# Side work of a second attention layer: the distance between users of one PSUM bank, by what reads the bank

## The chip, the cores and the metric

The kernel runs on one core of a Trainium2 chip. The metric is the device time of one execution in microseconds (us); lower is better. Given are three timed runs of the kernel before, and one execution that the hardware profiler recorded.

## The reference, cut to what matters

The program is a stack of four transformer layers over 2 sequences of 1024 tokens with 256 features: each layer normalises x, and adds an attention-like part and a feed-forward part to it. The change touches the attention of the second layer alone. It has 16 query heads of 128 dimensions and 4 key/value heads, rotary position embedding, a causal softmax, and a gate per token and head:

```python
q = (hidden_states @ Wq.T).reshape(b, sl, H, D)      # H = 16, D = 128
k = (hidden_states @ Wk.T).reshape(b, sl, HKV, D)    # HKV = 4
v = (hidden_states @ Wv.T).reshape(b, sl, HKV, D)
q = _rope(q, cos, sin); k = _rope(k, cos, sin)
...
scores = jnp.einsum('bhsd,bhtd->bhst', q, k) * scale   # causal
attn = jnp.einsum('bhst,bhtd->bhsd', jax.nn.softmax(scores, axis=-1), v)
out = (g * attn).transpose(0, 2, 1, 3).reshape(b, sl, H * D)
return out @ Wo.T
```

The reference also picks key blocks, but with 16 of 16 picked this does not alter the result, and the kernel leaves it out.

## The kernel before, in words

All matmuls are in fp32. The second attention runs over 8 groups: 2 sequences times 4 key/value heads, each with 4 query heads j. A group goes over 8 tiles of 128 query rows, qt, in the order 7, 0, 6, 1, 5, 2, 4, 3. One *unit* is one pair (qt, j), so there are 32 units in a group and 256 in all, and 7 more at the end that hold only what is left over.

In its unit a pair gets its **scores** on TensorE (PE): `scores()` multiplies 128 query rows with (qt+1)·128 keys into `sc`, a PSUM tile of two banks, of which there are two (`bufs=2`). `softmax()` then adds the causal mask on VectorE (DVE, L156), reduces the maximum there (L158), and takes the exponential with the row sum on ScalarE (ACT, L159), which is the last to read `sc`. A reciprocal on DVE (L666) and a multiplication by it and by the gate on GpSimd (POOL, L667) finish `pr`.

Two units behind the last of a qt's four pairs, `outputs()` begins to work it off: for each block of 128 keys a `turn` (four PE transposes of `pr` into the tile `tp`, L573, copied to `pT` by ACT or DVE in turn, L684) and a `product` (one matmul of 512 columns with v into `op`). These pieces are spread over four units; the first one or two are put ahead of a unit's scores (`early`), the rest behind them (`late`). The last product is followed by a copy of `op` to `oT` on ACT (L697), and queues the **output projection** of this qt: `project(oT)`, four matmuls of 256 columns with `w1o` into the bank m1, which one DVE addition to x reads (`add_to_x`, L134).

The **fills** are the side work: the 8 output projections of a group, and the 12 projections of the next group (2 key, 8 query, 2 value). All use one PSUM bank, m1, one after the other. A key or query projection (four matmul records of 512 columns) is read by three DVE operations (`rope`, L597, L599, L600), a value projection (16 records of 128 columns) by one copy on ACT (L632).

The order of all matmuls and transposes of this stage on PE is the order in which the code emits them (`keep_in_program_order`); the other engines' instructions are ordered by the tile scheduler. In each unit, `unit()` does: the unit's early pieces, the scores, at most one fill, and the unit's late pieces. `took` is the estimated PE time of scores and late pieces (0.22 a block of scores, 0.44 a turn, 0.86 a product). A fill is taken if there is one, if `owed`, the time left over against 3.5 a unit, is above zero, and if `since`, the sum of `took` since the last fill, is above 2.2. `since` contains the late pieces of the present unit, though they are emitted behind the fill. Output projections go to the head of the list of fills.

Of the kernel before, what the change touches and what calls it, by code (L numbers as in the profile page):

```python
# [46 lines left out]
def kernel(ctx: ExitStack, tc: tile.TileContext, a: dict, out: bass.AP):  # L47
# [85 lines left out]
    def add_to_x(i, ps):  # L133
        V.tensor_tensor(xs[i], ps, xs[i], ALU.add)  # L134
# [87 lines left out]
    with work_pool("l0") as pool, tc.tile_pool(  # L222
# [26 lines left out]
        def pe(out_, lhsT, rhs, first, last):  # L249
            tc.keep_in_program_order(PE.matmul(out_, lhsT=lhsT, rhs=rhs, start=first, stop=last))  # L250
# [4 lines left out]
        def bank():  # L255
            free.append(free.pop(0))
            return free[-1]
# [134 lines left out]
        def project(b, pair, qt):  # L392
            i = b * QT + qt
            yp = bank()[:, :D]
            for jp in range(2):
                pe(yp, os_[b, pair, jp][:, qt * P : (qt + 1) * P], wo0[:, 2 * pair + jp, :], jp == 0, jp == 1)
            add_to_x(i, yp)
# [32 lines left out]
        begun, soon, later = [], [], []  # L430
# [6 lines left out]
        owed = [0.0]  # L437
# [26 lines left out]
        for b, pair in pairs:  # L464
            for h in range(2):
                for g in (2 * pair, 2 * pair + 1):
                    for qt in range(4 * h, 4 * h + 4):
                        n = (qt + 1) * P
# [93 lines left out]
    with work_pool("l1") as pool, tc.tile_pool(  # L562
# [40 lines left out]
        groups = [(b, g) for b in range(B) for g in range(4)]  # L603
        kTs, qTs, vgs = {}, {}, {}

        def key(b, g, h):
            if (b, g) not in kTs:
                kTs[b, g] = pool.tile([P, T], F32, tag="k1", name=f"kT1_{b}_{g}")
            cols = slice(h * 512, (h + 1) * 512)
            kp = bank()  # L610
            for k in range(2):
                pe(kp, w1k[:, k, g * P : (g + 1) * P], xnT[2 * b + h][:, k, :], k == 0, k == 1)
            rope(kTs[b, g][:, cols], kp, cols, f"k{b}_{g}_{h}")

        def query(b, g, j, h):
            if (b, g, j) not in qTs:
                qTs[b, g, j] = pool.tile([P, T], F32, tag="q1", name=f"qT1_{b}_{g}_{j}", bufs=8)
            hc = slice((4 * g + j) * P, (4 * g + j + 1) * P)
            cols = slice(h * 512, (h + 1) * 512)
            qp = bank()  # L620
            for k in range(2):
                pe(qp, w1q[k][:, hc], xnT[2 * b + h][:, k, :], k == 0, k == 1)
            rope(qTs[b, g, j][:, cols], qp, cols, f"q{b}_{g}_{j}_{h}")
# [10 lines left out]
        def projections(b, g):  # L634
            return (
                [lambda h=h: key(b, g, h) for h in range(2)]
                + [lambda j=j, h=h: query(b, g, j, h) for j in range(4) for h in range(2)]
                + [lambda h=h: value(b, g, h) for h in range(2)]
            )
# [11 lines left out]
        with phase("l1_main") as main:  # L651

            def scores(b, g, qt, j):
                n = (qt + 1) * P
                i = b * QT + qt
                nm = f"1_{b}_{g}_{qt}_{j}"
                sc = main.tile([P, T], F32, tag="S", name=f"sc{nm}", bufs=2)
                for c in range(0, n, 512):
                    cols = slice(c, min(c + 512, n))
                    pe(sc[:, cols], qTs[b, g, j][:, qt * P : n], kTs[b, g][:, cols], True, True)  # L660
                long = n > 512
                pr = pool.tile([P, 512 * (1 + long)], F32, tag=f"pr{long}", name=f"pr{nm}", bufs=7)
                total = pool.tile([P, 1], F32, tag="total", name=f"total{nm}", bufs=4)
                softmax(pool, sc, n, pr[:, :n], total, nm)
                r = pool.tile([P, 1], F32, tag="r", name=f"r{nm}", bufs=4)
                V.reciprocal(r, total)  # L666
                G.tensor_scalar(  # L667
                    pr[:, :n], pr[:, :n], r, gate[:, i, 4 * g + j : 4 * g + j + 1],
                    op0=ALU.mult, op1=ALU.mult,
                )  # L670
                return pr

            def outputs(b, g, qt, prs):

                nm = f"1_{b}_{g}_{qt}"
                made = {}

                def turn(kb):
                    tp = main.tile([P, 4, P], F32, tag="T", name=f"tp{nm}_{kb}", bufs=2)
                    for j in range(4):  # L680
                        pe_t(tp[:, j, :], prs[j][:, kb * P : (kb + 1) * P])
                    made[kb] = pool.tile([P, 4, P], F32, tag="pT1", name=f"pT{nm}_{kb}", bufs=3)
                    with tc.high_priority():
                        (V.tensor_copy if kb % 2 else S.copy)(made[kb], tp)  # L684

                def product(kb):
                    if kb == 0:
                        made["op"] = main.tile([P, 4, P], F32, tag="O", name=f"op{nm}")
                    op = made["op"]
                    pe(  # L690
                        op.rearrange("p j q -> p (j q)"), vgs[b, g][:, kb, :],
                        made[kb].rearrange("p j q -> p (j q)"), kb == 0, kb == qt,
                    )
                    if kb == qt:
                        oT = pool.tile([P, 4, P], F32, tag="oT1", name=f"oT{nm}")
                        with tc.high_priority():
                            S.copy(oT, op)  # L697
                        soon.append((1.75, lambda: project(oT)))

                def project(oT):  # L700
                    yp = bank()[:, :D]
                    for j in range(4):
                        h = 4 * g + j
                        pe(yp, oT[:, j, :], w1o[h // 8][:, h % 8, :], j == 0, j == 3)
                    add_to_x(b * QT + qt, yp)

                pieces = [(0.44, lambda: turn(0))]
                for kb in range(qt + 1):
                    if kb < qt:
                        pieces.append((0.44, lambda kb=kb: turn(kb + 1)))  # L710
                    pieces.append((0.86, lambda kb=kb: product(kb)))
                return pieces

            early, late, soon, fills = {}, {}, [], []
            UNIT, owed, since, u = 3.5, 0.0, 0.0, 0

            def unit(make):
                nonlocal owed, since  # L720
                for _, work in early.pop(u, []):
                    work()
                took, pr = make()
                took += sum(cost for cost, _ in late.get(u, []))
                fills[0:0] = soon
                soon.clear()
                owed += UNIT - took
                since += took
                if fills and owed > 0 and since > 2.2:
                    cost, work = fills.pop(0)  # L730
                    owed -= cost
                    since = 0.0
                    work()
                for _, work in late.pop(u, []):
                    work()
                return pr

            for n, (b, g) in enumerate(groups):
                due = [(1.75, work) for work in projections(*groups[n + 1])] if n + 1 < len(groups) else []
                fills += due  # L740
                for qt in (7, 0, 6, 1, 5, 2, 4, 3):
                    prs = []
                    for j in range(4):
                        prs.append(
                            unit(lambda: (0.22 * (qt + 1), scores(b, g, qt, j)))
                        )

                        if u < NSLOT:
                            tc.keep_in_program_order(
                                nc.scalar.dma_start(out=sent[u * P : (u + 1) * P, :], in_=none)  # L750
                            )
                        u += 1
                    pieces = outputs(b, g, qt, prs)
                    cut = 1 + (qt > 0)
                    early[u + 2], pieces = pieces[:cut], pieces[cut:]
                    share = sum(cost for cost, _ in pieces) / 4
                    for m in range(4):
                        late[u + 2 + m] = []
                    at, used = u + 2, 0.0
                    for piece in pieces:  # L760
                        late[min(at + int(used / share), at + 3)].append(piece)
                        used += piece[0]
                while due and due[-1] in fills:
                    fills.pop(0)[1]()
            while early or late or soon or fills:
                unit(lambda: (2.5, None))
                u += 1
# [37 lines left out]
    with work_pool("l2") as pool, tc.tile_pool(  # L805
# [410 lines left out]
        for blk in range(N2 + 1):  # L1216
            for i in range(4):
                t, hs = i // 2, i % 2
                work = []
# [643 lines left out]
```

## Time and profile before

| | |
|---|---|
| Median of three runs | 3122.94 us (3121.41 to 3129.98) |
| Profiled execution: its time / its span | 3125.69 us / 3124.0 us |
| Second attention's main loop, within the span | 742 to 1656 us |
| PE busy in it | 885.65 us of 914 |
| DVE / ACT / POOL busy in it | 546.04 / 337.58 / 297.75 us |
| Mean granted clock of PE in the whole span / in this stage | 0.97 / 1.00 |
| Matmuls of this stage by kind: scores / products / transposes | 286.1 / 292.9 / 164.7 us |
| Output projections / query, value, key projections | 123.3 / 107.2, 27.9, 24.4 us |

A line of a timeline gives the start, the time, the engine, the line of the kernel, the operation, what it writes and reads, the shape and how many equal instructions follow one another; in square brackets stands how long the engine was idle before, and what ended that. An fp32 matmul shows as two records, so an output projection of four matmuls is "x8". The end of a matmul is modelled, and the next one starts some 0.15 us before it: the time that one takes from its neighbours is the distance between starts. A line of the waits gives who waited for whom, the total in us, how many times, and the longest. A line of stages gives the length, the busy time of each engine with its instruction count, the granted clock, the share of the DMA engines and GB/s.

### The profile page before, as it was taken

What the parts mean: (1) busy time and instruction counts of PE and PEld (TensorE: products, weight loads), DVE (VectorE), ACT (ScalarE), POOL (GpSimd) and SP (SyncE); (2) the same over time, 40 slices, a digit from 0 to 9 for tenths busy, and PEclk for the clock granted to TensorE, in tenths of its full rate; (3) what the DMA queues carried; (4) which work ended last, traced back from release to release, by engine and by line L of the source; (5) the groups of instructions that cost most, each with busy time, mean ns of one, the idle gap of its engine ahead of it and who ended that gap; (6) DMA issues with size and microseconds to landing.
All of it is one profiled execution on the core that took longest, in us unless ns stands there. A gap on an engine that the chain in (4) does not pass through costs nothing. (4 is left out here: it accounts for less than half of the span.)

```text
span 3124.0 us, 43744 instructions
## 1 busy us (share of the span) xinstructions
PE 2911.5 (93%) x16724; PEld 1976.3 (63%) x16724; DVE 1741.7 (56%) x3876; ACT 1194.8 (38%) x2122; POOL 923.1 (30%) x1274
## 2 busy tenths in 40 slices
PE   6999999989999999999999977999999999998798
PEld 5666666545655655655655555677777777655697
DVE  5765655326666666566551167677777775333223
ACT  2123333332333333333441144765766665222111
POOL 2021010103333333333320024444354443212462
PEclk9999999979999999999999988999999999999899
DMA  5000010001100000000000010000000000002496
GB/s 157 1 28 15 1 55 1 1 28 60 40 23 1 1 1 0 1 1 14 35 1 18 1 41 1 1 1 1 1 1 1 1 1 20 17 1 93 157 351 210
DMA packets 77203, 107.76 MB, mean 34 GB/s; under 512 B 7680, under 2 KB 60480, under 8 KB 75456
## 3 DMA queue, kind: packets, MB, share of 16 engines
q1 hardware_dynamic: 62160, 85.05, 8.4%
q10 hardware_dynamic: 11376, 10.41, 1.0%
q0 software_dynamic: 3456, 9.47, 0.8%
q8 instruction: 134, 2.20, 0.3%
q14 instruction: 77, 0.63, 0.1%
HBM read 82.94 MB, written 21.97 MB: 34 GB/s over the span
## 5 line engine op out<-in xcount | busy, mean ns | idle before, releaser
L159 ACT ACTIVATE pr<-sc,nmax 128x896 f32<-128x896 f32 (+7 forms) x272 | 201.3, 741 | 469.2 <-DVE nmax L158 372.3
L667 POOL TENSOR_SCALAR pr<-pr,r,gate 128x1024 f32<-128x1024 f32 (+7 forms) x256 | 209.9, 821 | 564.3 <-DVE r L666 535.3
L570 PE MATMUL sc<-kT,qT 128*128 128x512 f32 (+3 forms) x768 | 291.7, 491 | 22.3 <-ACT pr L159 22.3
L570 PE MATMUL op<-pT,v 128*128 128x512 f32 x576 | 292.9, 595 | 1.8 <-DVE pT L684 1.2
L344 ACT ACTIVATE pT<-sc 128x1024 f32<-128x1024 f32 (+1 forms) x160 | 150.1, 938 | 269.7 <-PE sc L250 269.6
L570 PEld LDWEIGHTS sc<-kT,qT 128*128 128x128 f32 x768 | 138.6, 192 | 156.9 <-issue 123.4
L158 DVE TENSOR_REDUCE nmax<-sc 128x1 f32<-128x896 f32 (+7 forms) x272 | 205.1, 757 | 8.0
L573 PEld LDWEIGHTS tp<-cst,pr 128*128 128x128 f32 x1152 | 140.7, 142 | 99.6 <-issue 70.4
L933 DVE SCALAR_TENSOR_TENSOR xp_ps<-xp,w2r,xp_ps 128x256 f32<-128x256 f32 x320 | 153.5, 486 | 60.3 <-ACT xp_ps L832 52.9
L250 PE MATMUL sc<-qk,qk 32*128 32x256 f32 (+1 forms) x1280 | 167.9, 379 | 9.4 <-ACT pT L344 8.8
L156 DVE TENSOR_TENSOR sc<-sc,cst 128x128 f32<-128x128 f32 x272 | 79.9, 296 | 172.5 <-PE sc L570 157.2
L958 POOL TENSOR_TENSOR dm<-cst,dA 128x512 f32<-128x512 f32 x128 | 133.3, 1050 | 116.2 <-PE lp L826 88.9
L347 POOL TENSOR_SCALAR_AFFINE_SELECT pT<-pT 128x512 f32<-128x512 f32 x64 | 40.6, 635 | 423.7 <-ACT pT L344 420.3
L573 PE MATMUL tp<-cst,pr 128*128 128x128 f32 x1152 | 164.7, 274 | 1.0 <-POOL pr L667 1.0
L250 PE MATMUL mx<-qk,qk 32*128 32x256 f32 (+1 forms) x1280 | 144.6, 387 | 10.8 <-DVE nm L319 3.0
L826 PE MATMUL lp<-dm,cst 128*128 128x512 f32 x256 | 137.1, 653 | 11.3 <-DVE ml L1023 6.4
L250 PEld LDWEIGHTS sc<-qk,qk 32*128 32x128 f32 x1280 | 104.1, 184 | 66.5 <-issue 31.2
L832 ACT ACTIVATE xp<-xp_ps,w2r 128x256 f32<-128x256 f32 x160 | 90.2, 564 | 128.3 <-PE xp_ps L826 104.4
L826 PE MATMUL xp_ps<-xnT,w2x 128*128 128x256 f32 x512 | 131.0, 402 | 7.3 <-DVE xx L933 3.9
L832 ACT ACT_TABLE_LOAD x105 | 134.7, 1283 | 3.7 <-PE zp L826 1.8
L684 ACT COPY pT<-tp 128x512 f32<-128x512 f32 x160 | 93.8, 586 | 106.2 <-PE tp L573 105.9
L826 PE MATMUL op<-w2o,xx 128*128 128x256 f32 x512 | 122.7, 389 | 5.1 <-DVE x L1166 3.7
(322 smaller groups left out, 5979.7 us busy)
## 6 DMA issues: line engine op xcount, KB each, us to landing
we<-in_L_W SPq DMA_DIRECT2D x80, 512.0 KB
sent<-none ACTq DMA_DIRECT2D x47, 129.0 KB
xg<-sent SPq DMA_DIRECT2D x40, 129.0 KB
gu<-in_L_gu SPq DMA_DIRECT2D x4, 1024.0 KB
back<-done SPq DMA_DIRECT2D x16, 256.0 KB
x<-in_x ACTq DMA_DIRECT2D x16, 128.0 KB
dn<-in_L_dn SPq DMA_DIRECT2D x2, 1024.0 KB
tabs<-in_L_rope SPq DMA_DIRECT2D x2, 1024.0 KB
```

Of the source, the lines that this page charges most:

```text
L158: V.tensor_reduce(nmax, sc[:, :n], axis=AX.X, op=ALU.max, negate=True)
L159: S.activation(pr, sc[:, :n], AF.Exp, bias=nmax, accum_out=total)
L250: tc.keep_in_program_order(PE.matmul(out_, lhsT=lhsT, rhs=rhs, start=first, stop=last))
L344: S.activation(pT[:, :, :, :w], sc[:, :, :, :w], AF.Exp, scale=0.25)
L570: tc.keep_in_program_order(PE.matmul(out_, lhsT=lhsT, rhs=rhs, start=first, stop=last))
L573: tc.keep_in_program_order(PE.transpose(out_, in_, ident))
L667: G.tensor_scalar(pr[:, :n], pr[:, :n], r, gate[:, i, 4 * g + j : 4 * g + j + 1], op0=ALU.mult, op1=ALU.mult,)
L684: (V.tensor_copy if kb % 2 else S.copy)(made[kb], tp)
L826: tc.keep_in_program_order(PE.matmul(out_, lhsT=lhsT, rhs=rhs, start=first, stop=last))
L832: tc.keep_in_program_order(S.activation(*args, **kw))
L933: V.scalar_tensor_tensor(dst[:, n] if k == 2 else pp[:, n], xp[:, n, k : k + 256], cw[:, c : c + 1], pp[:, n], op0=ALU.mult, op1=ALU.add,)
L958: G.tensor_tensor(dm, le.unsqueeze(1).to_broadcast([P, 4, P]), dAc[:, 4 * g : 4 * g + 4].unsqueeze(2).to_broadcast([P, 4, P]), ALU.mult,)
```

## The change

A fill now carries its own distance: behind an output projection of outputs the next fill may come once `since` is above 1.3, behind any other projection above 2.2 as before. The distance is set when a fill is taken, and holds for the fill after it. The costs, `owed` and the order of the list are not altered.

```diff
-                        soon.append((1.75, lambda: project(oT)))
+                        soon.append((1.75, lambda: project(oT), 1.3))
...
-            UNIT, owed, since, u = 3.5, 0.0, 0.0, 0
+            UNIT, owed, since, settled, u = 3.5, 0.0, 0.0, 2.2, 0
...
                 since += took
-                if fills and owed > 0 and since > 2.2:
-                    cost, work = fills.pop(0)
+                if fills and owed > 0 and since > settled:
+                    cost, work, settled = fills.pop(0)
                     owed -= cost
                     since = 0.0
                     work()
...
-                due = [(1.75, work) for work in projections(*groups[n + 1])] if n + 1 < len(groups) else []
+                due = [(1.75, work, 2.2) for work in projections(*groups[n + 1])] if n + 1 < len(groups) else []
```

More of the change, by code (lines that the diff above doesn't have):

```diff
@@ L716 @@
             early, late, soon, fills = {}, {}, [], []
-            UNIT, owed, since, u = 3.5, 0.0, 0.0, 0
+            UNIT, owed, since, settled, u = 3.5, 0.0, 0.0, 2.2, 0
             def unit(make):
-                nonlocal owed, since
+                nonlocal owed, since, settled
                 for _, work in early.pop(u, []):
```

## The prediction, made before the changed kernel ran

> **What bounds the kernel now.** I read the page first: TensorE (PE) is busy 93% of the span. Then the busy time by stage, for the second attention's main loop (742 to 1656 us), and what PE waits for in it.
>
> ```profile
> span 3124.0 us, 43744 instructions
> ...
> PE 2911.5 (93%) x16724; PEld 1976.3 (63%) x16724; DVE 1741.7 (56%) x3876; ACT 1194.8 (38%) x2122; POOL 923.1 (30%) x1274
> ```
>
> ```profile
> core 0: us, PE busy (x) PEld busy (x) DVE busy (x) ACT busy (x) POOL busy (x), PEclk, DMA share, GB/s
> 742.00:1656.00 914.00, 885.65 (x3500) 534.51 (x3500) 546.04 (x1165) 337.58 (x749) 297.75 (x326) 1.00 0.03 11
> ```
>
> ```profile
> PE sc L570 <- ACT pr L159: 22.3, 13, 2.3
> ```
>
> The stage is 914 us and PE works 885.65 of it: moving work between units can win back at most the 28.3 us of idle time. Of that, 22.3 us are score matmuls waiting for the exponential (L159) that reads the score buffer they need. The timeline of PE shows this wait once in each of the 8 groups, always 2.30 us: at 782.57, 900.41, 1018.34, 1134.58, 1250.82, 1367.07, 1483.31 and 1588.99, together 18.4 us. The third, in the timeline of PE:
>
> ```profile
> start us, us, engine line op out<-in xcount [idle before <-releaser]
> 1010.71 0.81 PE L570 MATMUL sc<-kT,qT 128*128 128x384 f32 x2
> 1011.36 1.89 PE L570 MATMUL m<-w1o,oT 128*128 128x256 f32 x8
> 1013.08 1.02 PE L570 MATMUL op<-pT,v 128*128 128x512 f32 x2
> 1013.94 2.10 PE L570 MATMUL sc<-kT,qT 128*128 128x512 f32 x6
> 1018.34 0.70 PE L570 MATMUL sc<-kT,qT 128*128 128x256 f32 x2 [2.30 <-ACT pr L159]
> 1018.87 1.89 PE L570 MATMUL m<-w1o,oT 128*128 128x256 f32 x8
> 1020.60 1.04 PE L573 MATMUL tp<-cst,pr 128*128 128x128 f32 x8
> ```
>
> In the code's order, with (qt, head) for the scores, this is: scores (6,2); output projection of qt 7; product of qt 0; scores (6,3) and, in the same row, scores (1,0); the gap; scores (1,1); output projection of qt 0; eight transposes of qt 6. The output projection of qt 0 stands right behind the gap.
>
> **What the change moves.** Nothing is added or removed: 148 fills before and after, with the same matmuls. Working `since` and `owed` through the 263 units of the loop by the code, with 1.3 in place of 2.2 behind an output projection, and in the compiled order of PE, seventeen fills change their unit:
> - In all 8 groups the output projection of qt 0 goes two units earlier (`since` is 1.54 there). On PE it now stands between scores (6,3) and scores (1,0), ahead of the gap.
> - In groups 1 to 6 the last value projection goes four units earlier (`since` 1.52), to behind scores (2,0). In group 0 both value projections and one output projection shift by one to four units.
>
> **Output projection of qt 0, group at 1018 us.** Scores (6,3) alone take 1.51 us (1011.36 less 1009.85, where the scores before it began), so the projection starts at 1013.94 + 1.51 = 1015.45. Its inputs are there: the copy to oT (L697) ended at 1014.73 and the bank's last reader, an addition of 0.42 us (L134), at 1013.70. It takes 1.72 us (1011.36 to 1013.08), to 1017.17; scores (1,0) follow, 0.44 us, to 1017.61. Scores (1,1) still wait for the exponential of (6,3), which ran from 1017.18 to 1018.19 and whose inputs on VectorE (DVE) lie ahead of everything that moves: 1018.34 again. So 0.73 us of the gap stays.
>
> Scores (1,1) take 0.53 us as before, to 1018.87, and now the eight transposes follow at once. Three of them (0.11 us each, 0.87 by 8) have their inputs; the fourth reads pr(6,3), which GpSimd (POOL) scales after the reciprocal r(6,3). On DVE the addition to x and the reduction of scores (1,0) stand ahead of that reciprocal. The addition starts 0.20 us behind the projection, at 1017.37; 0.42 later the mask addition, 0.34 to the reduction, 0.42 for that, less an overlap of 0.08 to 0.1: r(6,3) at 1018.45, against 1018.32 before. POOL begins 0.26 later and takes 1.09 (rows at 1018.32 and 1018.58), to 1019.80; the transpose starts 0.06 later, at 1019.86. Five transposes, 0.55, give 1020.41 for scores (1,2), which started at 1021.47: **1.05 us earlier**. The gap of 2.30 becomes two of some 0.7.
>
> Bounds for this term: the row of POOL ended pr(6,3) at 1019.67 even without the 0.13 of delay, so the fourth transpose cannot start before 1019.73, against 1020.93 before: 1.2 us at most. From below, nothing if POOL or DVE come a microsecond later. I take 1.05, worked out from the rows of the same spot.
>
> Behind scores (1,2) seven groups have a fill of 1.72 us ahead of the product that needs the first copy from PSUM, which covers ScalarE's (ACT's) copy. In the last group there is no such fill: ACT copies only after the exponential of (1,1), to about 1.4 us behind scores (1,1) plus 0.8 us, and the product waits some 0.3 us. I take 0.75 there. Sum: 7 x 1.05 + 0.75 = **8.1 us**.
>
> **The clock.** After the gap of group 1 the granted clock fell for one stretch, and the same projection and transposes took 2.66 and 1.62 us in place of 1.73 and 0.87: 1.7 us lost.
>
> ```profile
> 900.00:902.00 2.00, 1.59 (x7) 1.37 (x8) 0.96 (x4) 0.81 (x4) 1.09 (x1) 0.93 0.39 132
> 902.00:904.00 2.00, 2.00 (x7) 1.54 (x6) 0.31 (x2) 0.56 (x2) 1.11 (x2) 0.50 0.19 66
> ```
>
> With the gap cut in two, 1.1 to 1.5 us of idle time remain in any 3 us, and I count this dip as gone: **1.7 us**. Bounds: 0 (it comes back elsewhere) and 3.4 (an execution with two). [...]
>
> **The value projection.** At its new place the bank was read last by the addition behind the output projection of qt 6. `since` counts 1.52 there, but 0.86 of it is a product that comes after the fill: on PE only scores (2,0) lie between, 0.64 us, from 1046.22 to 1046.86, and the addition ran from 1046.42 to 1046.84. With 0.06 us to PE that is a wait of 0.04, times 7: 0.2 to 0.3 us. Behind it the scores and transposes of units 52 to 55 come 1.8 us later, and where it stood before, PE goes straight from scores (4,0) to a transpose and the product of (5,3). Its copy on DVE would end at 1058.1, the product start at 1059.1 (on the clock of before): a margin of 1.0 us, and the last group, which has no value projections, runs this spot at 1621 without a wait. Queues: the ACT copy of v moves ahead of one oT copy, and ends 2 us before its reader. POOL is passed by nothing. On SP's queue the load of the next layer's w2r waits for the slot that the last value projection frees (it was issued at 1523.74), and goes earlier with it; the load behind it waits until 1656 in any case. So **-0.2 us**.
>
> **Sum.** 8.1 + 1.7 - 0.2 = 9.6 us. The second SwiGLU behind the stage starts when PE is done, and its last weights (dn) were issued at 1456 for a first use at 1684; the state-space layer's w2x were issued at 1498 for 1848. Later stages hang on PE and on transfers that they issue themselves, so the gain is kept to the end. The profiled execution took 3125.69 us (span 3124.0) and would take 3116.1; it lies 2.75 above the median of the three runs, 3122.94, from which 9.6 gives **3113.3 us**. The bound of 0.3% is 9.4 us, about what a measurement of this kernel can tell from no change: the forecast lies on it.
>
> **Rivals.**
> - *The gap re-forms at the transposes* (some 0 to 0.5 us a group stay): 8 x 0.25 = 2 us, 3121; with the clock's 1.7, 3119. For it: pr(6,3) comes out of DVE, ACT and POOL in turn, and the change puts an addition ahead of the reciprocal. Against: the timetable above has to be wrong by 0.5 us. [...]
> - *All that the rows allow*: 1.2 us in each group, and two dips of the clock less: 8 x 1.2 + 3.4 = 13 us, 3110.
> - *Slower, by the clock*. Two shorter gaps close together trip the clock in place of one. For it: three gaps of 1.01, 1.00 and 0.60 us between 747.7 and 751.9 us went with a mean clock of 0.69 from 750 to 754. Against: they held 2.6 us of idle time within 4.2, the new ones hold at most 1.5. Each dip costs 1.7; with two in each group, 16 less the one that is there, 25.5 - 7.9 = 17.6 us slower, 3140.5. From 6 dips on the gain is gone, from 12 on the kernel is slower by over 0.3%.
> - *The move doesn't happen*: excluded, the order of PE shows it.
>
> **How the numbers follow.** Forecast 0.66, its own range 3109 to 3118 (1.2 to 0.8 us a group, 0 to 3.4 of clock); a little more than half of it lies beyond 9.4 us. Re-formed gap 0.13, all within 0.3%. All that the rows allow 0.12. Slower 0.09. Faster by over 0.3%: 0.38 + 0.12 = 0.50; within: 0.28 + 0.13 = 0.41; slower: 0.09. Later stages too have stretches at half clock (0.50 from 1832 to 1840), which can shift by one or two either way at 1.7 us each; with the bounds above the range is 3106 to 3122.
>
> **What would show it.** PE's wait for L159 falls from 22.3 us to about 9; the rows at the eight places show the projection ahead of the short scores and a wait of about 0.6 before (1,1) and of about 0.6 before a transpose, released by POOL (L667, which now holds 1.0 us of PE's waits). No stretch under 1.00 between 889 and 1007. PE's wait for bank m at the value projection stays under 0.1 each. The forecast is wrong if the transposes wait over 1.2 us, if the products of qt 5 wait for DVE, or if the clock dips in more than two groups.

## The result and the profile after

The changed kernel took 3112.8 us (median of 11 runs, 3101.4 to 3118.1) against 3122.94 for the kernel before beside it (11 runs). The ratio is 0.9965, with a 95% interval of 0.9954 to 0.9977. By the medians that is 10.1 us less, by the ratio 10.9, with 7 to 14 as its interval. The profiled execution took 3109.01 us, its span is 3107.3, against 3125.69 and 3124.0.

The page, the stage of the main loop (same columns as before) and PE's waits in it:

```profile
span 3107.3 us, 43752 instructions
...
PE 2906.0 (94%) x16724; PEld 1970.6 (63%) x16724; DVE 1741.9 (56%) x3876; ACT 1197.0 (39%) x2122; POOL 923.1 (30%) x1274
```

```profile
742.00:1656.00 914.00, 894.24 (x3518) 535.69 (x3517) 548.21 (x1168) 343.03 (x754) 297.86 (x326) 1.00 0.04 13
```

```profile
PE sc L570 <- ACT pr L159: 8.5, 13, 1.0
PE tp L573 <- POOL pr L667: 5.1, 9, 1.0
PE m L570 <- DVE t2q L600: 3.2, 6, 0.6
```

PE's wait for the exponential fell from 22.3 us to 8.5, and a wait for POOL grew from 1.0 to 5.1: 13.8 us gone and 4.1 come, 9.7 less in all. (The stage row has the bounds of before; its last 6 us now belong to the SwiGLU.) The third group in the timeline of PE shows how:

```profile
1011.28 1.02 PE L570 MATMUL op<-pT,v 128*128 128x512 f32 x2
1012.14 1.67 PE L570 MATMUL sc<-kT,qT 128*128 128x512 f32 x4
1013.64 1.89 PE L570 MATMUL m<-w1o,oT 128*128 128x256 f32 x8
1015.37 0.59 PE L570 MATMUL sc<-kT,qT 128*128 128x256 f32 x2
1016.53 0.70 PE L570 MATMUL sc<-kT,qT 128*128 128x256 f32 x2 [0.57 <-ACT pr L159]
1017.07 0.49 PE L573 MATMUL tp<-cst,pr 128*128 128x128 f32 x3
1018.07 0.77 PE L573 MATMUL tp<-cst,pr 128*128 128x128 f32 x5 [0.51 <-POOL pr L667]
1018.67 0.60 PE L570 MATMUL sc<-kT,qT 128*128 128x256 f32 x2
```

The output projection stands ahead of scores (1,0); the gap of 2.30 us has become one of 0.57 before scores (1,1) and one of 0.51 before the fourth transpose. All eight groups show the same two waits. From scores (1,1) to scores (1,2) it is 2.14 us (1016.53 to 1018.67), against 3.13 before (1018.34 to 1021.47): 0.99 less. The waits of a group shrink by more, 2.30 - 0.57 - 0.51 = 1.22 us. A wait is counted from the modelled end of the matmul ahead of it, some 0.15 us behind the point at which the next one would have started, so the second wait hides that much again; and the first transpose behind it takes 0.05 longer than the others. DVE at the same place:

```profile
1015.57 0.42 DVE L134 TENSOR_TENSOR x<-m,x 128x256 f32<-128x256 f32 x1 [0.30 <-PE m L570]
1016.00 0.30 DVE L156 TENSOR_TENSOR sc<-sc,cst 128x128 f32<-128x128 f32 x1
1016.33 0.42 DVE L158 TENSOR_REDUCE nmax<-sc 128x1 f32<-128x256 f32 x1
1016.67 0.15 DVE L666 RECIPROCAL r<-total 128x1 f32<-128x1 f32 x1
```

The addition to x is now ahead of the reciprocal r(6,3), which begins 0.14 us behind scores (1,1), where before it began 0.02 ahead of them.

The main loop, from scores (7,2) of the first group (at 742.07 and 743.97 us) to the first matmul of the SwiGLU behind it, took 914.53 us before and 905.62 after. For the comparisons below, a *step* is the time from scores (1,1) of one group to those of the next:

| kernel | first step | the next five | last step | scores (1,1) of the last group to SwiGLU |
|---|---|---|---|---|
| before | 117.84 | 117.93, 116.24, 116.24, 116.25, 116.24 | 105.68 | 67.61 |
| after | 116.96 | 115.38 each | 104.81 | 66.74 |

The 117.93 of before holds the stretch at half clock (0.50) that the prediction showed, 3.41 us long (901.71 to 905.12 us), worth 117.93 - 116.24 = 1.69 us. The trace of after has no such stretch behind any of the eight gaps (the clock is 1.00 from 756.3 to 1817.8 us); the same place, 901 to 905 us:

```profile
901.00:903.00 2.00, 1.34 (x8) 1.00 (x9) 1.24 (x5) 0.92 (x5) 1.27 (x2) 1.00 0.35 117
903.00:905.00 2.00, 2.00 (x10) 1.24 (x8) 1.40 (x4) 0.84 (x4) 0.92 (x2) 1.00 0.20 66
```

The two profiled executions differ by 16.7 us, more than the medians. The loop gives 8.9 of it; ahead of it the changed kernel was 1.9 us the slower. Behind the loop the program took 1467.4 us before and 1457.7 after, with PE at half clock for 126.5 and 102.4 us of it, in stages that the change does not touch. On another chip a second pair (the repeats below) took 1439.7 and 1436.3 us there, with a mean granted clock of 0.97 in both. A stretch of 3.41 us at half clock cost 1.69 us above, so the 24.1 us of difference in the first pair are worth up to 12 us, by estimate. I put this part down to the scatter of the executions; no run separates it.

### The profile page after: what moved, and what is told of

It is laid out like the page before. It is cut to its first block, busy times and chain, and to the rows that moved or that the text cites. A ratio compares the mean times of both kernels' runs of the same rounds, so it can differ in the third digit from the quotient of the medians.

```text
span 3107.3 us, 43752 instructions
## 1 busy us (share of the span) xinstructions
PE 2906.0 (94%) x16724; PEld 1970.6 (63%) x16724; DVE 1741.9 (56%) x3876; ACT 1197.0 (39%) x2122; POOL 923.1 (30%) x1274
## 5 line engine op out<-in xcount | busy, mean ns | idle before, releaser
L159 ACT ACTIVATE pr<-sc,nmax 128x896 f32<-128x896 f32 (+7 forms) x272 | 201.4, 741 | 459.2 <-DVE nmax L158 384.1
L667 POOL TENSOR_SCALAR pr<-pr,r,gate 128x1024 f32<-128x1024 f32 (+7 forms) x256 | 210.0, 821 | 555.5 <-DVE r L666 554.4
```

The lines of the kernel that those rows point to most:

```text
L159: S.activation(pr, sc[:, :n], AF.Exp, bias=nmax, accum_out=total)
L667: G.tensor_scalar(pr[:, :n], pr[:, :n], r, gate[:, i, 4 * g + j : 4 * g + j + 1], op0=ALU.mult, op1=ALU.mult,)
```

## The experiments

The theory was the prediction's: the output projection of qt 0, moved ahead of the gap, brings all of the gain that is not clock, and the value projection brings none. The rivals: the value projection's move matters, too; a shorter distance is better in general; what is left of the gap can be filled in the same way. Diffs are against the changed kernel unless said otherwise. The unmodified kernels ran beside the experiments on each chip; the chips differ (medians of before 3119.1, 3094.8 and 3096.2 us), so that only ratios and steps are compared across them.

**The output projection alone.** The shorter distance holds only behind the output projection of qt 7, which is the one before qt 0's; the value projections stay where they were before.

```diff
-                        soon.append((1.75, lambda: project(oT), 1.3))
+                        soon.append((1.75, lambda: project(oT), 1.3 if qt == 7 else 2.2))
```

> The output projection of qt 0 goes two units earlier in all 8 groups, and nothing else moves (1.3 only behind the output projection of qt 7, 2.2 elsewhere). Theory (the gain comes from the score gap and the clock dip behind it, the value projection costs a little): the wait for L159 falls to 8 to 9 us and L667 holds about 5, as in the changed kernel, and a steady group, from one restart of the scores (1,1) to the next, takes 115.25 us, against 116.24 before and 115.38 in the changed kernel: 0.99 less than before in each. Time against before 0.996 to 0.998, 0 to 1.5 us better than the changed kernel. Rival (the moved value projection carries part of the gain): a steady group takes 115.6 us or more and the time lies between the two kernels.

Measured: 3105.33 us, ratio 0.9965 (0.9951 to 0.9979), the same as for the whole change. The steps from group 1 on are 115.24 to 115.25 us, 0.99 to 1.00 less than before, and PE's waits are those of after (8.6 us for L159, 5.1 for POOL). The one move carries the whole gain.

**The value projection alone.** A waiting output projection now always needs 2.2, so that the one of qt 0 stays behind the gap; only a waiting projection of the next group may come at 1.3, and of these only the value projections do (`fills[0][2]` is the distance that the waiting fill carries, 1.3 for output projections).

```diff
-                if fills and owed > 0 and since > settled:
+                if fills and owed > 0 and since > (settled if fills[0][2] > 2 else 2.2):
```

> Only the value projections (and one output projection in group 0) go earlier; the output projection of qt 0 stays behind the gap. Theory: the gap of 2.30 us stays in all 8 groups, PE's wait for L159 stays at 22 us, and a steady group takes 116.24 + 0.13 = 116.37 us; the time against before is 1.000 to 1.001. The clock falls to 0.50 behind one gap in three to eight. Rival (the value projection helps): a steady group under 116.2, ratio 0.999 or less.

Measured: 3119.69 us, ratio 1.0002 (0.9989 to 1.0014). The gaps of 2.30 us are all there (L159: 22.2 us of PE's waits). The steps without a clock dip are 116.38, 0.14 more than before. So the value projection costs 0.14 a group and gains nothing. This trace has two dips at half clock, behind the gaps of groups 1 and 5 (mean clock 0.53 from 905 to 907 us, 0.50 from 1373 to 1375). The first, in the timeline of PE:

```profile
904.29 0.70 PE L570 MATMUL sc<-kT,qT 128*128 128x256 f32 x2 [2.30 <-ACT pr L159]
904.83 3.35 PE L570 MATMUL m<-w1o,oT 128*128 128x256 f32 x8
907.97 1.20 PE L573 MATMUL tp<-cst,pr 128*128 128x128 f32 x7
```

The output projection takes 3.35 us here and 1.89 elsewhere. Both dips lengthen their steps, to 118.07 and 118.05, by 1.67 to 1.69.

**A still shorter distance.** With 0.8 behind every output projection the next group's query projection comes one place earlier, behind scores (1,1), where it covers the second short gap.

```diff
-                        soon.append((1.75, lambda: project(oT), 1.3))
+                        soon.append((1.75, lambda: project(oT), 0.8))
```

> The distance behind an output projection is 0.8 in place of 1.3: a query projection then goes into the second gap, ahead of the eight transposes that wait 0.51 us for POOL, and the projections behind it go one to three units earlier. Theory (the bank's readers set the limit): the wait of the transposes is gone, but the next query projection comes only 1.3 us of PE behind the first (eight transposes and one short score) and waits about 1.7 us for the three DVE operations of the rope and a copy between them; a steady group takes about 116.5 us, and the time is back near that of before, 0.999 to 1.001. Rival (the second gap is the cost, the counter's distance is long enough): a steady group takes 114.8, ratio to before 0.995 or less.

Measured: 3119.05 us, ratio 1.0003 (0.9992 to 1.0013): all of the gain is gone. The steps from group 1 on are 116.54 to 116.56. PE's longest waits in the loop, and the third group on PE and on DVE:

```profile
PE m L570 <- DVE t2q L600: 14.3, 13, 1.6
PE sc L570 <- ACT pr L159: 8.3, 13, 1.0
```

```profile
1019.75 1.88 PE L570 MATMUL m<-xnT,w1q 128*128 128x512 f32 x4
1021.47 1.04 PE L573 MATMUL tp<-cst,pr 128*128 128x128 f32 x8
1022.34 0.60 PE L570 MATMUL sc<-kT,qT 128*128 128x256 f32 x2
1024.52 1.98 PE L570 MATMUL m<-xnT,w1q 128*128 128x512 f32 x4 [1.58 <-DVE t2q L600]
```

```profile
1021.67 0.69 DVE L597 TENSOR_TENSOR qT<-m,tabs 128x512 f32<-128x512 f32 x1
1022.37 0.69 DVE L599 TENSOR_TENSOR t2q<-m,tabs 64x512 f32<-64x512 f32 x1
1023.08 0.69 DVE L684 COPY pT<-tp 128x512 f32<-128x512 f32 x1
1023.78 0.68 DVE L600 TENSOR_TENSOR t2q<-m,tabs 64x512 f32<-64x512 f32 x1
```

The second short gap is gone: the eight transposes no longer wait for POOL, and the wait of 0.57 ahead of scores (1,1) stays as it was. But the next query projection now follows closely behind the first. The bank is free only when the last of three rope operations has read it, and a copy of pT stands between them on DVE: 2.8 us from 1021.67 to 1024.46, where an output projection's reader takes 0.42. The wait has moved from the score tile to the bank.

**The same with that next projection held back.** Behind the output projection of qt 0 the distance is 0.8, and the query projection that then comes carries 2.7, so that the one after it comes one unit later.

```diff
-                        soon.append((1.75, lambda: project(oT), 1.3))
+                        soon.append((1.75, lambda: project(oT), {7: 1.3, 0: 0.8}.get(qt, 1.3)))
...
-                due = [(1.75, work, 2.2) for work in projections(*groups[n + 1])] if n + 1 < len(groups) else []
+                due = [(1.75, work, 2.7 if m == 7 - (n == 0) else 2.2) for m, work in enumerate(projections(*groups[n + 1]))] if n + 1 < len(groups) else []
```

> As the changed kernel, but the one query projection behind the gap goes one unit earlier, ahead of the eight transposes (distance 0.8 behind the output projection of qt 0), and the next one is held where it was (distance 2.7 behind this one). Theory: the transposes find pr(6,3) done, their wait of 0.51 us and the slow restart of 0.07 go, and neither the bank nor ACT's copy makes PE wait: a steady group takes 114.8 us against 115.38, the time is 3 to 4 us below the changed kernel's, ratio to before 0.995 to 0.996. Rival (the query projection was the cover of the first product of qt 6): the product waits 0.5 us or more for the copies on ACT and DVE, and a steady group takes 115.3 us or more.

Measured: 3109.88 us, ratio 0.9975 (0.9964 to 0.9986). The trace follows the theory: steps of 114.88 (114.73 in group 1), 0.50 less than after, PE's wait for POOL down to 1.5 us, none at the bank beyond after's. The time does not show it, and the expected 0.995 to 0.996 was missed: the ratio lies above that of the output projection alone, with intervals that overlap. The four kernels so far ran together; the kernels before and after and this one were therefore run again, on another chip, beside a fifth.

**The changed kernel again**, unmodified:

> The changed kernel once more, on one chip with the three that follow. A steady group takes 115.38 us, the gaps are 0.57 and 0.51, and no stretch under a clock of 1.00 lies behind a gap between 770 and 1650 us. Ratio to before 0.9955 to 0.9975.

Measured: 3084.65 us, ratio 0.9969 (0.9955 to 0.9982). Steps of 115.39.

**The held-back version again**, unmodified:

> The version with the query projection in the second gap, once more, beside the changed kernel. Its main loop is 3.9 us shorter by the traces (901.75 against 905.62 us from the first scores to the first matmul of the SwiGLU). Theory (what the loop wins stays to the end, and the later stages scatter by the clock): 3 to 5 us below the median of after_again, or by chance of the clock within 4 us of that. Rival (the later stages take it back each time): no faster than after_again, by 1 us or more slower, and the stretch behind the loop is again longer than in the changed kernel.

Measured: 3080.94 us, ratio 0.9958 (0.9942 to 0.9973), 3.7 us below the changed kernel beside it. The steps are the same as the first time (114.88). The intervals overlap. From the first scores (1,1) to the last it is 794.84 us here and 798.74 in the changed kernel: 3.9 us.

**Half of the second gap in another way.** With 1.9 behind the output projection of qt 7, the output projection of qt 0 goes one place earlier than before instead of two: scores (1,0) come ahead of it, and scores (6,3) and (1,0) run back to back.

```diff
-                        soon.append((1.75, lambda: project(oT), 1.3))
+                        soon.append((1.75, lambda: project(oT), 1.9 if qt == 7 else 2.2))
```

> The output projection of qt 0 goes one unit earlier, not two: into the gap, but behind the short scores (1,0) and not ahead of them (1.9 behind the output projection of qt 7, 2.2 elsewhere). DVE then has the mask and the reduction of (1,0) done before the addition to x, and the reciprocal of (6,3) is no longer delayed. Theory (0.16 us of the second gap are the delay of that reciprocal): the wait for POOL falls from 0.51 to 0.35, a steady group takes 115.08 us, against 115.24 with the projection ahead of the short scores. Rival (the second gap is POOL's and ACT's time alone): 115.24, wait 0.51. If the projection filled the whole gap at no price: 114.5.

Measured: 3082.74 us, ratio 0.9954 (0.9939 to 0.9970). The third group in the timeline of PE:

```profile
1013.28 2.10 PE L570 MATMUL sc<-kT,qT 128*128 128x512 f32 x6
1015.22 1.89 PE L570 MATMUL m<-w1o,oT 128*128 128x256 f32 x8
1017.68 0.70 PE L570 MATMUL sc<-kT,qT 128*128 128x256 f32 x2 [0.57 <-ACT pr L159]
1018.21 0.49 PE L573 MATMUL tp<-cst,pr 128*128 128x128 f32 x3
1019.07 0.76 PE L573 MATMUL tp<-cst,pr 128*128 128x128 f32 x5 [0.36 <-POOL pr L667]
```

On DVE the reduction of scores (1,0) now comes ahead of the addition to x, the reciprocal r(6,3) starts 0.02 us ahead of scores (1,1) again (1017.66), and the second wait is 0.36 in place of 0.51, as expected. Scores (1,2) follow scores (1,1) by 1.99 us instead of 2.14. But only the step of group 1 keeps that (115.10); from group 2 on the steps are 115.23, 0.01 below the output projection alone. The second query projection, two fills later, reaches the bank 0.03 us too early and takes 1.82 us from its neighbours instead of 1.72, which gives 0.13 of the 0.15 back. So this expectation was half met: the wait shrank, and the step did not.

**The kernel before again**, unmodified, as a measure of the comparison:

> The kernel before, once more: what the comparison gives for no change. Ratio 0.999 to 1.001. A steady group takes 116.24 us where the clock holds; behind one to three of the eight gaps of 2.30 us the clock falls to 0.50 and costs 1.7 us each (theory: the gap trips the clock). Rival (the dip of the first profile was a chance that has nothing to do with the gap): no dip between 770 and 1650 us, or dips away from the gaps.

Measured: 3093.44 us, ratio 0.9992 (0.9983 to 1.0002). Its trace repeats that of before: the gaps of 2.30, steps of 116.24, and one clock dip, again behind the gap of group 1 (0.50 from 902 to 904 us; a step of 117.93).

**Both good moves, without the value projection's.** As the held-back version, with 2.2 behind all other output projections.

```diff
-                        soon.append((1.75, lambda: project(oT), 1.3))
+                        soon.append((1.75, lambda: project(oT), {7: 1.3, 0: 0.8}.get(qt, 2.2)))
...
-                due = [(1.75, work, 2.2) for work in projections(*groups[n + 1])] if n + 1 < len(groups) else []
+                due = [(1.75, work, 2.7 if m == 7 - (n == 0) else 2.2) for m, work in enumerate(projections(*groups[n + 1]))] if n + 1 < len(groups) else []
```

> Both gaps filled and the value projection left where it was: 1.3 behind the output projection of qt 7, 0.8 behind that of qt 0 with the next query projection but one held at 2.7, 2.2 elsewhere. By the steps measured so far a steady group takes 114.88 - 0.14 = 114.74 us, 1.50 less than before and 0.64 less than in the changed kernel, and the loop is 4 to 5 us shorter than the changed kernel's. Theory (the loop's gain stays to the end): 4 us below the changed kernel's median on the same chip, give or take 3 for the clock of the later stages; ratio to before 0.994 to 0.9965. Rival (the later stages take back what goes beyond the change): no faster than the changed kernel, 0.9965 or more.

Measured: 3078.83 us, ratio 0.9944 (0.9922 to 0.9965), the lowest ratio of all versions, though the intervals of the next ones overlap with it. The third group in the timeline of PE:

```profile
1009.06 1.89 PE L570 MATMUL m<-w1o,oT 128*128 128x256 f32 x8
1010.78 0.59 PE L570 MATMUL sc<-kT,qT 128*128 128x256 f32 x2
1011.95 0.70 PE L570 MATMUL sc<-kT,qT 128*128 128x256 f32 x2 [0.57 <-ACT pr L159]
1012.49 1.88 PE L570 MATMUL m<-xnT,w1q 128*128 128x512 f32 x4
1014.20 1.04 PE L573 MATMUL tp<-cst,pr 128*128 128x128 f32 x8
1015.08 0.60 PE L570 MATMUL sc<-kT,qT 128*128 128x256 f32 x2
```

The query projection covers the time in which POOL finishes pr(6,3), and the eight transposes run without a wait. The second of the two short gaps is gone, in all groups but the last, which has no query projection left. Steps of 114.73 (114.58 in group 1).

**The changed kernel beside it**, unmodified:

> The changed kernel a third time, as the partner of the version with both gaps filled. A steady group 115.38 us, no dip of the clock behind a gap, ratio to before 0.9955 to 0.9975.

Measured: 3083.78 us, ratio 0.9964 (0.9949 to 0.9980), 5.0 us above the version that leaves the value projection out and fills both gaps. Steps of 115.38. From the first scores (1,1) to the last it is 798.71 us here and 793.83 there: 4.9 us, the difference of the medians. By the ratios alone the intervals still overlap.

## Why the prediction was right

The forecast was 3113.3 us and 3112.8 was measured. That is closer than its terms were, and the closeness is luck: the interval of the measured gain is 7 us wide, and the sum of 9.6 us stands against 8.9 in the loop of the profiled pair, of which 2.0 are the clock, and how often that falls differs between executions (behind one, one and two of the eight gaps in the three traces with the gap of 2.30 us). Point by point:

- **Only idle time can be won, and it is the gap.** Right. The waits of PE on L159 fell to 8.5 us, where about 9 was forecast, and PE's other waits in the loop, POOL's apart, are those of before.
- **The order.** Right, as the trace shows it: scores (6,3), projection, scores (1,0), a wait for the same exponential, scores (1,1), three transposes, a wait for POOL (L667). The two waits were put at about 0.6 each and are 0.57 and 0.51.
- **The addition to x delays the reciprocal r(6,3).** Right: it starts 0.14 us behind scores (1,1), 0.11 was forecast, and where the projection goes one place later, behind scores (1,0), the second wait is shorter by 0.15.
- **1.05 us a group: 0.99.** The term was 0.06 too large. Most of it is the five transposes behind the wait, which I put at 0.55 and which take 0.60 (1018.07 to 1018.67); the reciprocal is 0.03 later than forecast. Over seven groups that is 0.4 us.
- **0.75 in the last group: 0.87.** The product does wait, but scores (1,2) to product take 0.54 us there (1584.99 to 1585.53) where 0.43 is usual: 0.11 and not the 0.3 that I took.
- **Value projection, -0.2 us: -0.9.** The term that was mis-sized most. The wait was put at 0.04, and it is 0.03 (0.67 us from the scores to the projection in the rows below, where 0.64 is usual); but the wait is not all of the price. After's row at the new place:

```profile
1158.79 0.81 PE L570 MATMUL sc<-kT,qT 128*128 128x384 f32 x2
1159.46 2.05 PE L570 MATMUL m<-w1kv,xnT 128*128 128x128 f32 x16
1161.35 1.02 PE L570 MATMUL op<-pT,v 128*128 128x512 f32 x2
```

  From 1159.46 to 1161.35 the sixteen records take 1.89 us. Where it stood before they took 1.79 (1056.79 to 1058.58 in the third group). With the 0.03 that is 0.13 a group, and the value projection alone measured 0.14. The prediction counted only the wait, though the trace of before had a row for a fill that arrives just too early. It is the first value projection of the same group:

```profile
1035.26 1.46 PE L570 MATMUL sc<-kT,qT 128*128 128x512 f32 x4
1036.57 2.05 PE L570 MATMUL m<-w1kv,xnT 128*128 128x128 f32 x16
1038.46 1.88 PE L570 MATMUL op<-pT,v 128*128 128x512 f32 x4
```

  The bank's last reader ended at 1036.51, the projection starts 0.01 to 0.02 us later than the rows ahead of it would have let it (1.31 us behind the start of the scores, where 1.29 is usual), and it takes 1.89 (1036.57 to 1038.46). Nor is this a price of the bank alone. Scores (1,1), which waited 2.30 us before and 0.57 after, take 0.53 and 0.54 to the next start (1018.34 to 1018.87, 1016.53 to 1017.07); scores (1,2), which did not wait, take 0.44 and 0.43. The single records of the trace show the extra 0.10 us in the first one behind the wait each time: 0.32 in place of 0.22 for scores (1,1), 0.21 in place of 0.11 for the value projection. So the extra 0.10 us stands behind waits of 0.03, 0.57 and 2.30 us alike; behind the 0.51 us for POOL the fourth transpose takes 0.05 more (0.16 in place of 0.11).
- **The clock, 1.7 us: 1.69 in this pair.** The dip of before cost what was forecast and is gone. In the traces with the gap of 2.30 us (before, its repeat, the value projection alone) it came 4 times behind 24 gaps; in the nine traces without that gap, never at the same place of their 72 groups. At 1.7 us each that makes 1.7 to 3.4 us in each of the three executions with the long gaps, and none in those without.
- **Kept to the end.** Right: the output projection alone, the value projection alone and the version with both good moves differ from before in the whole time as their steps do, within the intervals. The first run of the held-back version is the weakest case: its steps alone, without any clock, are worth 10.7 us, a ratio of 0.9966, and it measured 0.9975 (0.9964 to 0.9986); its repeat gave 0.9958.

Sum by the rows: 7 x 0.99 + 0.87 - 7 x 0.13 + 1.69 = 8.6 us, and 0.3 at the loop's start, ahead of the first gap. That is the clock again: both traces have a stretch at half clock there (from 751.52 us before, from 752.87 after), and it covers 2.48 us of the first query projection before and 1.93 after. Half of the difference is 0.27, and the projection takes 2.95 and 2.68 us. Of the rivals, a re-formed gap and a slower clock are excluded by the traces, and "all that the rows allow" by the 0.99. The slower rival had two short gaps trip the clock more often than one long one; it was the other way round.

The length of a single wait does not settle whether a dip follows. Of the 24 gaps of 2.30 us, 20 were followed by none, nor was the wait of 1.58 to 1.59 us for bank m that the version with the still shorter distance has in seven groups. At the loop's start two waits of 1.01 and 1.00 us (scores at 748.69, transposes at 750.51) came ahead of the stretch that begins at 751.52 us in the trace of before. The one dip behind a gap in that trace cost 1.69 us, which is the prediction's term; no run shows what decides which gap gets one.

What stays open: why the first matmul record behind a wait takes 0.05 to 0.10 us longer, and what decides whether a gap is followed by a dip. No experiment here is made for either.

## What to carry to other kernels

Space the users of a shared buffer by what reads it: here, behind a reader of 0.42 us, the next one could come two units earlier (ratio 0.9965 for that move alone), and a next one close behind readers of 2.8 us cost the whole gain again (1.0003). Of several moves that one rule makes, look which one closes a gap on the bounding engine and make that alone; the others ride along and can cost (0.14 us a group for the value projection). When a gap is filled, look at once for the next late input (here pr from POOL) and for a second piece of work that can stand in front of it.

## What was not expected of the hardware

- Behind some of the gaps of 2.30 us the clock fell: in the three traces with these gaps 4 of 24 were followed by a stretch at half clock, 3.41 us long in the trace of before, and each cost 1.67 to 1.69 us. The other 20 were followed by none, and nothing here shows what sets the four apart.
- Matmuls that had to wait took up to 0.10 us longer than the same ones that did not: behind 0.01 to 0.03 us for a bank (1.89 us against 1.79 for a value projection, 1.82 against 1.72 for a query projection in the run with half of the second gap) as behind 2.30 us for an exponential (0.53 against 0.44 for scores (1,1)), and 0.05 us for the transposes behind 0.51 us for POOL. For the arrivals that were 0.01 to 0.03 us too early, this price was at least three times the wait.
- The stretches at half clock in the later stages add up to 126.5 us in the profiled execution of before and to 102.4 us in that of after, in stages that the change does not touch. By estimate that difference is worth up to 12 us, as much as the change brings (10.1 us by the medians), so that the step in the loop (repeatable to 0.01 us) tells more than the time of one execution.
